# First chunk's projections and delta inside the stage ahead of each scan, and x kept by channels between scan layers

## The chip, the cores and the metric

The kernel runs on one core of one Trainium2 chip. The metric is the device time of one execution in microseconds (us). A core has five engines that each work through a queue of their own: TensorE (PE, with its weight loads as PEld), VectorE (DVE), ScalarE (ACT), GpSimd (POOL) and SyncE (SP), which here issues nearly all DMA transfers.

## What is computed

The input x has 4 images of 64 x 64 pixels with 96 channels. Two layers of a state-space model (layers 0 and 1) and two layers of linear attention with a quantised feed-forward network (layers 2 and 3, the token layers) follow each other, all with residuals:

```
x = x + conv(gn(x))          # layers 0 and 1; gn: mean and variance per group of 3 channels
t = t + attn(ln(t)); t = t + ffn(ln(t))    # layers 2 and 3

conv(v):                                   # D_INNER = 192, D_STATE = 16, K = 4 directions
  xp, z = split(v @ in_proj)               # 96 -> 2 * 192
  u  = silu(depthwise_conv3x3(xp) + bias)
  xs = u by rows, by columns, and both of these reversed
  dt, B, C = split(x_proj[k] @ xs[k])      # 6, 16 and 16 rows
  delta = softplus(dt_proj[k] @ dt + dt_bias[k])
  h[t] = exp(delta * A) * h[t-1] + (delta * u) * B[t]     # 16 states
  y[t] = sum over states of h[t] * C[t] + D * u
  y  = layernorm(sum of the 4 directions in image order) * w + b
  return (y * silu(z)) @ out_proj          # 192 -> 96
```

## The kernel before

**Units.** The images go in pairs, so each of layers 0 and 1 makes two units, four in all. The 192 inner channels of two images fill three groups of 128 partitions: `u0` and `u1` hold the first 128 channels of image 0 and 1, and `u2` the other 64 of both. For each unit `between_scans` runs a stage that makes the unit's `u` and, beside it, turns the scan's result of the unit before into x (`scan_outputs`). Then `scan_pair` runs the scan. After the fourth unit `token_layers` makes the last unit's outputs and layers 2 and 3.

**The stage.** `scan_inputs` is a generator. `turn(i)` (L171) loads image i in 8 pieces `xt` of 512 tokens, turns each by four TensorE transposes into `tps`, copies it to `xn` (ACT, L183) and takes its statistics (`bn_stats`, DVE, L184). Two tiny matmuls `gm` and `gv` sum them over a group of channels. `project(i, c)` (L202) then works on 512 tokens: the norm on VectorE in place (L207), three matmuls `ips` (L211; each shows as two records in the trace), copies into a padded image `img` and into `zs`, which is stored as `zg`. The convolution is split. `conv_product` (L144) does 512 positions by 9 matmuls `cps` with diagonal weights, and `conv_chain` (L155) does 1024 positions by 9 steps on VectorE (one `tensor_scalar`, L164, and eight `scalar_tensor_tensor`, L166), each with a SiLU on ScalarE. There are 8 products (18 records each in the trace) and 8 chains in a stage:

```
    for c in range(8):
        project(1, c)
        if c in (2, 5, 7):
            conv_chain(0, {2: 0, 5: 16, 7: 32}[c])
    for n in range(8):
        conv_product(*((1, 8 * n) if n < 6 else (0, 8 * n)))
        if n % 2:
            conv_chain(2, 8 * n - 8)
    conv_chain(1, 48)
```

**The outputs.** `scan_outputs` (L243) works on 16 groups of 256 tokens of both images. It loads `zt`, `ys` and the residual `xr`, takes layer norm statistics (`ystats`, `ymv` on DVE; the inverse root `ln_rs` on POOL, L81), normalises on ACT, transposes (`pt`, L292), scales (`gt`, ACT, L294), multiplies with silu(z) (`gt`, DVE, L301), multiplies with the output weights (`po`, L305 and L306), adds the residual (`xo`, DVE, L308) and stores. Two steps of `scan_inputs` follow each group.

**Order.** In stages and token layers a scheduler orders each engine's queue from the instructions' dependences and estimated costs. Within a scan the written order is kept: `InOrder` passes each instruction through L71, which is why the trace shows L71 for all of them.

**The scan.** `scan_pair` (L326) works on chunks of T = 1024 positions: 4 directions, 4 chunks, 3 partition groups, 48 steps. For each chunk `project` makes `xps` (x_proj), its copy `cdt`, the DRAM rows `crow`, `bt`, and a split of B in three bf16 parts (`parts`, `rest`, `bparts`). For each step `discretise` makes `delta` (softplus), `du` = delta * u (POOL) and its transpose `dut`. Both run ahead of the steps that need them, in between the scan's own work. Only for the first chunk nothing runs ahead, and before the loop stands (L602):

```
        for _ in begin_project(0, 0):
            pass
        for _ in begin_discretise(0):
            pass
```

The scan's own work is `da` = exp(delta * A) (ACT), `bp` (PE, DVE), the scan instruction `h` (DVE), `h` times the broadcast rows `cb` (POOL; `cb` and `bb` come by DMA from `crow`), and the sum `yp` (PE).

Of the kernel before, what the change touches and what calls it, by code (L numbers as in the profile page):

```python
# [84 lines left out]
class ScanLayer:  # L85


    def __init__(self, tc, pw, dram, ident, x_src, x_dst, w, n):
        nc = tc.nc
        self.x_src, self.x_dst, self.w = x_src, x_dst, w  # L90

        self.zg = [dram.tile([3, 128, L], F32, name=f"zg{n}{pr}") for pr in range(NB // 2)]
        self.y = [dram.tile([2, L, DI], F32, name=f"y{n}{pr}") for pr in range(NB // 2)]
        self.par = par = pw.tile([128, 2, P_ALL], F32, name=f"par{n}")
        nc.sync.dma_start(out=par, in_=w["par"].rearrange("s p c -> p s c"))

        self.amat = pw.tile([128, 2, K * NS], F32, name=f"amat{n}")
        nc.scalar.activation(self.amat, par[:, :, P_A : P_A + K * NS], AF.Exp)
        nc.vector.tensor_scalar(self.amat, self.amat, -1.0, None, ALU.mult)
        self.dsum = pw.tile([128, 2, 1], F32, name=f"dsum{n}")  # L100
        nc.vector.tensor_reduce(self.dsum, par[:, :, P_D : P_D + K], mybir.AxisListType.X, ALU.add)


def between_scans(tc, cst, ident, half, u, before, after):


    with ExitStack() as stage:
        ins = scan_inputs(tc, stage, cst, ident, half, u, *after)
# [10 lines left out]
def scan_inputs(tc, stage, cst, ident, half, u, layer, pr):  # L119
# [49 lines left out]
    xns, norms = [], []  # L169

    def turn(i):  # L171

        xn = pa.tile([C, L], F32, name="xn", tag=f"xn{i}")
        xns.append(xn)
        stats = p2.tile([C, 8, 6], F32, name="stats")
        for g in range(8):
            xt = p2.tile([128, 4, C], F32, name="xt")
            at = (2 * pr + i) * L + g * 512
            nc.sync.dma_start(out=xt, in_=x_src[at : at + 512, :].rearrange("(j p) c -> p j c", p=128))
            ps = pp.tile([C, 512], F32, name="tps", tag="mm")  # L180
            for j in range(4):
                nc.tensor.transpose(ps[:, 128 * j : 128 * j + 128], xt[:, j], ident)
            nc.scalar.copy(xn[:, 512 * g : 512 * g + 512], ps)  # L183
            nc.vector.bn_stats(stats[:, g], ps)  # L184
# [17 lines left out]
    def project(i, c):  # L202
# [4 lines left out]
        nc.vector.tensor_scalar(xns[i][:, cols], xns[i][:, cols], *norms[i], ALU.subtract, ALU.mult)  # L207
        pss = []
        for q in range(3):
            ps = pp.tile([128, 8, HW], F32, name=f"ips{q}", tag="mm")  # L210
            nc.tensor.matmul(ps, wi[:, i, 128 * q : 128 * q + 128], xns[i][:, cols], start=True, stop=True)  # L211
# [10 lines left out]
    for i in range(2):  # L222
        yield from turn(i)
    for c in range(8):
        project(0, c)
        if c % 2:
            yield
    for c in range(8):
        project(1, c)
        if c in (2, 5, 7):  # L230
            conv_chain(0, {2: 0, 5: 16, 7: 32}[c])
        if c % 2:
            yield
    for n in range(8):
        conv_product(*((1, 8 * n) if n < 6 else (0, 8 * n)))
        if n % 2:
            conv_chain(2, 8 * n - 8)
        yield
    conv_chain(1, 48)
    yield  # L240


def scan_outputs(tc, stage, ident, half, layer, pr, pp, turned="pt", summed="po"):  # L243
# [3 lines left out]
    p2 = stage.enter_context(tc.tile_pool(name="c2", bufs=3))  # L247
# [3 lines left out]
    for g in range(NT // 2):  # L251
# [3 lines left out]
        xr = p2.tile([128, 2, 2, C], F32, name="xr")  # L255
# [3 lines left out]
        for i, to, of in (  # L259
# [6 lines left out]
            )  # L266
        for i in range(2):
            there = (2 * pr + i) * L + at
            nc.sync.dma_start(
                out=xr[:, :, i], in_=x_src[there : there + 256, :].rearrange("(t p) c -> p t c", p=128)  # L270
            )
# [30 lines left out]
        po = pp.tile([128, 2, 2, C], F32, name="po", tag=summed, bufs=1 if summed == "po" else None)  # L302
        for t in range(2):
            for i in range(2):
                nc.tensor.matmul(po[:, t, i], gt[:, i, t], wo[:, 0], start=True, stop=False)  # L305
                nc.tensor.matmul(po[:, t, i], gt[:, 2, t], wo[:, 1 + i], start=False, stop=True)  # L306
        xo = p2.tile([128, 2, 2, C], F32, name="xo")
        nc.vector.tensor_tensor(xo, xr, po, ALU.add)  # L308
        for i in range(2):
            there = (2 * pr + i) * L + at  # L310
            nc.sync.dma_start(
                out=x_dst[there : there + 256, :].rearrange("(t p) c -> p t c", p=128), in_=xo[:, :, i]
            )
# [12 lines left out]
def scan_pair(tc, pk, cst, ident, u, first_weights, layer, pr):  # L326

    nc = InOrder(tc)
    par, amat, dsum, w, y = layer.par, layer.amat, layer.dsum, layer.w, layer.y[pr]
    with ExitStack() as stage:  # L330
        p2 = stage.enter_context(tc.tile_pool(name="b_2", bufs=2))
        pm = stage.enter_context(tc.tile_pool(name="b_ps", bufs=1, space=PSUM))
        pd = stage.enter_context(tc.tile_pool(name="b_d", bufs=2, space=DRAM))

        sel, ident16 = cst["sel"], cst["ident16"]

        def part(t, tr, c):

            v = t.rearrange("p (h w) -> p w h", w=HW) if tr else t.rearrange("p (h w) -> p h w", w=HW)
            return v[:, 16 * c : 16 * c + 16]  # L340

        weights = {0: first_weights}
# [5 lines left out]
        def project(k, uv):  # L348


            wx = weights[k][0]
            bparts = p2.tile([NP, T], BF16, name="bparts")
            cdt = p2.tile([NC, T], F32, name="cdt")
            crow = pd.tile([ND, T], F32, name="crow")
            bt = p2.tile([128, T // 128, 2 * NS], F32, name="bt")
            projected.append((uv, bparts, crow, cdt, bt))
            for hf in range(2):
                for j in range(3):
                    yield hf, 8 + 2 * j
                    if j == 0:  # L360
                        ps = pm.tile([NC, 512], F32, name="xps", tag="m1")
                    nc.tensor.matmul(ps, wx[:, j], uv[j][:, 8 * hf : 8 * hf + 8], start=(j == 0), stop=(j == 2))
                yield hf, 14
                nc.scalar.copy(cdt[:, 512 * hf : 512 * hf + 512], ps)
            nc.sync.dma_start(out=crow, in_=cdt[:ND])
            yield 2, 6
            ps = pm.tile([128, T // 128, 2 * NS], F32, name="btps", tag="m1")
            for t in range(T // 128):
                nc.tensor.transpose(ps[:, t], cdt[BR, 128 * t : 128 * t + 128], ident[BR, BR])

            parts = p2.tile([128, T // 128, 3, 2 * NS], BF16, name="parts", bufs=1)
            rest = p2.tile([128, T // 128, 2 * NS], F32, name="rest", bufs=1)
            yield 2, 8
            nc.scalar.copy(bt, ps)
            nc.scalar.copy(parts[:, :, 0], ps)
            nc.vector.tensor_tensor(rest, ps, parts[:, :, 0], ALU.subtract)
            yield 2, 10
            nc.scalar.copy(parts[:, :, 1], rest)
            yield 2, 10
            nc.gpsimd.tensor_tensor(parts[:, :, 2], rest, parts[:, :, 1], ALU.subtract)  # L380
            yield 2, 12
            ps = pm.tile([NP, T], BF16, name="bpps", tag="m1")
            for t in range(T // 128):
                nc.tensor.transpose(
                    ps[:, 128 * t : 128 * t + 128], parts[:, t].rearrange("p s n -> p (s n)"), ident16
                )
            yield 2, 14
            nc.scalar.copy(bparts, ps)
            yield None

        def discretise(k, j, uv, cdt):

            wdt = weights[k][1]
            bias = par[:, j // 2, P_DTB + k : P_DTB + k + 1]
            delta = p2.tile([128, T], F32, name="delta")
            du = p2.tile([128, T], F32, name="du")
            dut = p2.tile([128, T // 128, 128], F32, name="dut")
            made.append((delta, du, dut))
            halves = [slice(512 * hf, 512 * hf + 512) for hf in range(2)]
            pss = []  # L400
            for hf, cols in enumerate(halves):
                yield 2 * hf
                ps = pm.tile([128, 512], F32, name="dps", tag=f"m{hf}")
                nc.tensor.matmul(ps, wdt[ND:, j], cdt[ND:, cols], start=True, stop=True)
                pss.append(ps)
            yield 4
            for ps, cols in zip(pss, halves):
                nc.scalar.activation(delta[:, cols], ps, AF.Softplus, bias=bias)
            yield 6
            nc.gpsimd.tensor_tensor(  # L410
                du.rearrange("p (a b) -> p a b", b=HW), delta.rearrange("p (a b) -> p a b", b=HW), uv[j], ALU.mult
            )
            for hf in range(2):
                yield 10 + 2 * hf
                ps = pm.tile([128, 4, 128], F32, name="dups", tag="m0")
                for t in range(4):
# [614 lines left out]
```

## Time and profile before

| what | value |
|---|---|
| median of 3 runs | 10735.83 us (10733.38 to 10756.34) |
| the profiled execution's own time | 10738.98 us |
| its span in the trace | 10737.1 us |
| busy in the span | PE 76%, DVE 89%, ACT 82%, POOL 84% |
| stage ahead of the first scan | 0 to 168.2 us |
| stages between scans | 2473.1 to 2714.4, 5005.4 to 5250.2, 7543.1 to 7786.2 us |
| token layers, with the last unit's outputs | 10081 to 10737 us |

A stage between scans is counted from the last `h` product of a scan to the first scan instruction of the next. PEclk is the share of full TensorE clock that was granted. In the views shown below, a line gives start, duration, engine, source line, operation and tiles; `x8` is a count of instructions. A chain of waits is the thread of work and waits that ended last in a window, followed back from its end.

### The profile page before, as it was taken

The page shows a single profiled execution, that of the slowest core. Times are in us where ns is not written, and L with a number is a line of the kernel's source. Part 1 is how long each engine was busy: PE and PEld are TensorE (multiplying, and loading weights), DVE is VectorE, ACT ScalarE, POOL GpSimd, SP SyncE. Part 2 cuts the span into 40 slices and gives each one's busy share as a digit, 9 for nine tenths or more (in the row PEclk, how much of TensorE's full clock was granted, in tenths as well). Part 3 has the DMA queues.
Part 4 walks back from the last instruction along what each step waited for, and adds up shares of the span by engine and source line. Part 5 has one row for each costly group of instructions (what it writes and reads, how often), then busy time and mean ns, then how long its engine had stood idle before and what let it go on. Part 6 is the DMA issues. An engine that isn't in the chain of part 4 may idle for free.

```text
span 10737.1 us, 143300 instructions
## 1 busy us (share of the span) xinstructions
PE 8117.2 (76%) x48032; PEld 6033.3 (56%) x48032; DVE 9607.7 (89%) x6898; ACT 8780.3 (82%) x18807; POOL 9031.2 (84%) x5306
## 2 busy tenths in 40 slices
PE   7777777777777777776877777777777777777666
PEld 4555555554555555555555555555455555555554
DVE  7999999997899999998799999999699999999755
ACT  6988888885888888886788888888598888888656
POOL 3999999993899999996499999999299999999645
PEclk9888899888888898998888888898888889889877
DMA  3677777775577777777467777777566777777610
GB/s 123 208 211 216 215 225 218 214 217 149 187 209 218 217 220 222 217 220 193 150 207 210 221 217 220 223 215 219 142 195 212 212 216 220 222 217 216 187 32 24
DMA packets 960474, 2114.19 MB, mean 197 GB/s; under 512 B 413526, under 2 KB 704664, under 8 KB 762008
## 3 DMA queue, kind: packets, MB, share of 16 engines
q1 hardware_dynamic: 959736, 2105.01, 67.6%
q8 instruction: 382, 6.26, 0.3%
q14 instruction: 356, 2.92, 0.1%
HBM read 1943.27 MB, written 161.48 MB: 196 GB/s over the span
## 4 chain that ended last, share of the span: by engine, by line
ACT 35%; PE 19%; DVE 18%; issue 18%; POOL 8%; DMA 1%; SPq 1%; DVEq 0%; POOLq 0%; ACTq 0%
ACT x L71 15%; ACT da L71 13%; DVE h L71 10%; PE yp L71 6%; POOL h L71 5%; PE bp L71 5%; DVE bp L71 4%; ACT bp L71 2%; DVE u L166 2%; PE xps L71 2%; PE dps L71 1%; ACT L71 1%; PE dups L71 1%; DMA cb<-crow 1%; PE cps L150 1%
## 5 line engine op out<-in xcount | busy, mean ns | idle before, releaser
L71 POOL TENSOR_TENSOR h<-h,cb 128x1024 f32<-128x1024 f32 x3072 | 7194.5, 2366 | 233.3 <-issue 59.8
L71 DVE TENSOR_TENSOR_SCAN h<-da,last,bp 128x1024 f32<-128x1024 f32 x2064 | 4736.7, 2335 | 145.6 <-PE bp L71 23.6
L71 ACT ACTIVATE x<-dut,bt 128x128 f32<-128x128 f32 x12288 | 3495.2, 370 | 1.3 <-PE bp L71 0.8
L71 PE MATMUL yp<-ident,h 128*128 128x128 f32 x24576 | 3357.2, 296 | 10.2 <-POOL h L71 10.2
L71 PEld LDWEIGHTS yp<-ident,h 128*128 128x128 f32 x24576 | 3183.8, 156 | 125.3 <-issue 74.5
L71 ACT ACTIVATE da<-delta,amat 128x1024 f32<-128x1024 f32 x2752 | 3060.2, 1138 | 97.5 <-DVE h L71 96.4
L71 PE MATMUL bp<-ident,x 128*128 128x128 f32 x10240 | 1678.2, 316 | 1290.8 <-DVE h L71 938.6
L71 PEld LDWEIGHTS bp<-ident,x 128*128 128x128 f32 x10240 | 1361.5, 163 | 1851.0 <-ACT x L71 1036.8
L71 DVE TENSOR_TENSOR bp<-du,bp 128x1024 f32<-128x1024 f32 x1472 | 1780.3, 1213 | 311.2 <-PE bp L71 309.2
L71 DVE TENSOR_TENSOR_SCAN h<-da,bp 128x1024 f32<-128x1024 f32 x688 | 1537.7, 2274 | 48.0 <-ACT da L71 8.5
L71 PE MATMUL bp<-bparts,sel 96*128 96x512 bf16 x2944 | 922.0, 399 | 759.1 <-DVE h L71 745.8
L71 PEld LDWEIGHTS <-sel 96*128 96x128 bf16 x2944 | 227.3, 100 | 1553.6 <-DVE h L71 1045.3
L71 ACT ACTIVATE bp<-delta,amat 128x1024 f32<-128x1024 f32 x320 | 358.1, 1119 | 527.9 <-DVE h L71 525.9
L71 POOL TENSOR_TENSOR dbu<-du,bb 128x1024 f32<-128x1024 f32 x320 | 755.2, 2360 | 0.0
L81 POOL TENSOR_TENSOR ln_rs<-ln_ve,half 128x4 f32<-128x4 f32 x64 | 89.7, 1402 | 575.5 <-DVE ln_ve L79 539.0
L71 DVE TENSOR_TENSOR_SCAN h<-bp,last,dbu 128x1024 f32<-128x1024 f32 x240 | 558.9, 2329 | 13.8 <-POOL dbu L71 12.5
L71 PE MATMUL xps<-u,wx 128*76 128x512 f32 x768 | 561.9, 821 | 5.7 <-ACT cdt L71 2.9
L71 POOL TENSOR_TENSOR du<-delta,u 128x1024 f32<-128x1024 f32 x192 | 506.2, 2637 | 21.6 <-ACT delta L71 21.6
L71 POOL COPY last<-h 128x2 f32<-128x2 f32 x1152 | 216.8, 188 | 346.6 <-DVE h L71 344.3
L71 ACT ACT_TABLE_LOAD x384 | 492.7, 1283 | 6.9
L71 PE MATMUL dps<-cdt,wdt 12*128 12x512 f32 x768 | 449.3, 666 | 0.0
L71 ACT COPY ysum<-yp 128x1024 f32<-128x1024 f32 x192 | 194.4, 1013 | 292.5 <-PE yp L71 292.5
(132 smaller groups left out, 6482.2 us busy)
## 6 DMA issues: line engine op xcount, KB each, us to landing
cb<-crow SPq DMA_DIRECT2D x1024, 1024.0 KB
cb<-crow SPq DMA_DIRECT2D x1024, 512.0 KB
bb<-crow SPq DMA_DIRECT2D x384, 256.0 KB
bb<-crow SPq DMA_DIRECT2D x128, 512.0 KB
y<-ysum SPq DMA_DIRECT2D x192, 256.0 KB
kept<-y SPq DMA_DIRECT2D x160, 256.0 KB
y<-ysum SPq DMA_DIRECT2D x64, 512.0 KB
zt<-zg SPq DMA_DIRECT2D x64, 384.0 KB
```

The lines of the kernel that those rows point to most:

```text
L71: return self.tc.keep_in_program_order(getattr(self.engine, op)(*args, **kwargs))
L81: nc.gpsimd.tensor_tensor(rs, ve, half, ALU.pow)
L150: nc.tensor.matmul(ps, diag[:, tap], v, start=(tap == 0), stop=(tap == 8))
L166: nc.vector.scalar_tensor_tensor(to, v, weight, to, ALU.mult, ALU.add)
```

## The change

`scan_pair` becomes a class `PairScan`. Its method `begin` makes the first chunk's `project` and the first step's `discretise` within `scan_inputs`, after two of the eight products and two of the eight chains, with the stage's PSUM buffers and under the scheduler. The tiles that even chunks and steps use live in a pool `s_q` that stays open from unit to unit; the odd ones are in a pool of the scan, one buffer each. `crow` too lives outside.

Between the layers x is kept as [image, channel, token]; the host hands it over so. `turn` becomes `measure`: `xt` is loaded as 96 channels x 512 tokens in two buffers, without transposes and copies, and is only measured. `project` loads the same piece again as `xn`, two buffers. In the outputs, `xr` comes by one transfer, `po` has channels on partitions (4 matmuls of 256 columns; the old 8 of 96), and one store is made. Layer 1's outputs are still by tokens, as the token layers want them: there `po` keeps its 8 matmuls, and four transposes add `xr` into it, so that a copy on ScalarE takes the place of the addition on VectorE. The outputs' tiles have two buffers (three before), but for the last unit.

```diff
-    def turn(i):
-        xn = pa.tile([C, L], F32, name="xn", tag=f"xn{i}")
...
+    def measure(i):
         stats = p2.tile([C, 8, 6], F32, name="stats")
         for g in range(8):
-            xt = p2.tile([128, 4, C], F32, name="xt")
...
-            for j in range(4):
-                nc.tensor.transpose(ps[:, 128 * j : 128 * j + 128], xt[:, j], ident)
-            nc.scalar.copy(xn[:, 512 * g : 512 * g + 512], ps)
-            nc.vector.bn_stats(stats[:, g], ps)
+            xt = p2.tile([C, 512], F32, name="xt", bufs=2)
+            nc.sync.dma_start(out=xt, in_=x_src[2 * pr + i, :, 512 * g : 512 * g + 512])
+            nc.vector.bn_stats(stats[:, g], xt)
...
-        nc.vector.tensor_scalar(xns[i][:, cols], xns[i][:, cols], *norms[i], ALU.subtract, ALU.mult)
+        xn = p2.tile([C, 512], F32, name="xn", bufs=2)
+        nc.sync.dma_start(out=xn, in_=x_src[2 * pr + i, :, cols])
+        nc.vector.tensor_scalar(xn, xn, *norms[i], ALU.subtract, ALU.mult)
...
     for c in range(8):
         project(1, c)
-        if c in (2, 5, 7):
-            conv_chain(0, {2: 0, 5: 16, 7: 32}[c])
+        if c == 2:
+            conv_chain(0, 0)
+        elif c == 5:
+            conv_chain(2, 0)
         if c % 2:
             yield
-    for n in range(8):
+    conv_product(1, 0)
+    conv_product(1, 8)
+    scan.begin(nc, pp)
+    yield
+    for n in range(2, 8):
         conv_product(*((1, 8 * n) if n < 6 else (0, 8 * n)))
-        if n % 2:
-            conv_chain(2, 8 * n - 8)
         yield
-    conv_chain(1, 48)
-    yield
+        conv_chain(*((0, 16), (0, 32), (2, 16), (2, 32), (2, 48), (1, 48))[n - 2])
+        yield
...
-    p2 = stage.enter_context(tc.tile_pool(name="c2", bufs=3))
+    p2 = stage.enter_context(tc.tile_pool(name="c2", bufs=3 if layer.last and pr else 2))
...
+        if not layer.last:
+            po = pp.tile([C, 2, 256], F32, name="po", tag=summed, bufs=bufs)
             for i in range(2):
-                nc.tensor.matmul(po[:, t, i], gt[:, i, t], wo[:, 0], start=True, stop=False)
-                nc.tensor.matmul(po[:, t, i], gt[:, 2, t], wo[:, 1 + i], start=False, stop=True)
...
+                for q, j in ((0, i), (1 + i, 2)):
+                    v = gt[:, j].rearrange("p t q -> p (t q)")
+                    nc.tensor.matmul(po[:, i], wo[:, q], v, start=(q == 0), stop=(q > 0))
+            xo = p2.tile([C, 2, 256], F32, name="xo")
+            nc.vector.tensor_tensor(xo, xr, po, ALU.add)
...
+        else:
...
+                    v = xr[:, i, 128 * t : 128 * t + 128]
+                    nc.tensor.matmul(po[:, t, i], v, ident[:C, :C], start=False, stop=True, is_transpose=True)
+            xo = p2.tile([128, 2, 2, C], F32, name="xo")
+            nc.scalar.copy(xo, po)
...
+    def begin(self, nc, pm):
+        for _ in self.project(nc, self.pq, pm, "mm", 0, 0):
+            pass
+        for _ in self.discretise(nc, self.pq, pm, ("mm", "mm"), 0):
+            pass
...
-        for _ in begin_project(0, 0):
-            pass
-        for _ in begin_discretise(0):
-            pass
```

## Prediction

> **What bounds the kernel now.** I read the page first (whole-kernel shares), then busy time over windows I chose for the stretches ahead of each scan, then the chain of waits in them. The page says that VectorE is busy 89%, GpSimd 84%, ScalarE 82% of the span; that belongs to the four scans, some 2300 us each, whose instructions the change leaves as they are, in the same written order. What moves lies in five windows: the stage ahead of the first scan (0 to 168.2 us), the three stages between scans (each from the last work of a scan to the first `h` scan of the next) and the token layers, where the last unit's outputs are made.
>
> ```profile
> core 0: us, PE busy (x) PEld busy (x) DVE busy (x) ACT busy (x) POOL busy (x), PEclk, DMA share, GB/s
> 0.00:168.20 168.20, 136.60 (x354) 64.11 (x354) 105.92 (x123) 70.86 (x114) 11.41 (x31) 0.96 0.31 91
> 2473.10:2714.40 241.30, 188.09 (x722) 108.61 (x722) 151.49 (x310) 124.21 (x240) 37.58 (x43) 0.86 0.49 138
> ...
> 7543.10:7786.20 243.10, 190.34 (x722) 110.59 (x722) 151.58 (x308) 124.19 (x240) 37.54 (x43) 0.85 0.49 137
> 10081.00:10737.00 656.00, 428.82 (x2928) 341.43 (x2928) 353.56 (x1252) 388.69 (x897) 299.18 (x362) 0.74 0.17 52
> ```
>
> First number: length of the window; then each engine's busy time. TensorE (PE) is the fullest engine in all of them, but no window is full. The chain of waits of 0 to 175 us (start, duration, what) says why:
>
> ```profile
> 38.27 44.10 PE ips L211 x96
> 82.37 61.82 PE cps L150 x144
> ...
> 144.96 2.81 PE xps L71 x6
> ...
> 153.43 0.44 DVE rest L71
> ...
> 159.77 2.35 POOL du L71
> ...
> 165.71 1.28 ACT L71
> 166.99 0.01 issue
> 167.00 1.15 ACT da L71
> ```
>
> TensorE runs unbroken from 38.3 to 144.2: in-projection, then the matmul half of the convolution. Then the first chunk's prologue (`xps` to `dut`, a table load, `da`) runs as one thread from hand to hand, 144.2 to 168.2. The VectorE half of the convolution ended at 128.9 and its engine then waits 24.5 us.
>
> A stage between scans has three phases. To 2542 us it is bound by latency: scan drain, `y` stores and the first output groups, about 12.8 us each. Then TensorE and VectorE are full together; last comes the prologue:
>
> ```profile
> 2552.00:2664.00 112.00, 109.95 (x366) 56.06 (x365) 104.79 (x171) 70.39 (x136) 17.25 (x9) 1.00 0.50 139
> ```
> ```profile
> 2688.00:2714.40 26.40, 16.31 (x42) 6.38 (x42) 1.69 (x4) 9.53 (x14) 3.00 (x2) 0.63 0.45 157
> ```
>
> In the second row only 16 of 26.4 us of TensorE are busy (at clock 0.63) and VectorE does 1.7 us. Prices for the full phase come from the groups of 2552 to 2664 (count, busy and mean ns):
>
> ```profile
> L166 DVE SCALAR_TENSOR_TENSOR u<-img,par,u 128x1024 f32<-128x1024 f32 x64 | 80.7, 1277 | 0.0
> L150 PE MATMUL cps<-img,diag 128*128 128x512 f32 x129 | 57.0, 593 | 0.0
> L81 POOL TENSOR_TENSOR ln_rs<-ln_ve,half 128x4 f32<-128x4 f32 x9 | 17.2, 1916 | 95.6 <-DVE ln_ve L79 83.4 <-ACT gt L294 8.4 <-ACT zs L217 3.7
> ```
>
> Records overlap, so I price by spacing: a tap on VectorE 1.20 us (64 of them fill 76.8 of the 112), a `cps` record 61.82/144 = 0.43, an `ips` record 44.1/96 = 0.46.
>
> **What the Trainium skill says.** "TensorE: Matmul & The Clock Gate", "Part 1: The HAM clock gate", puts an idle array at half clock and asks about 3.4 us of sustained work to release it: the trace shows 1.00 in the full phase and 0.63 over the prologue. "Part 4: PE-mode transpose" there gives about 275 ns for a transpose within a kernel; here a `pt` record took 0.27 us in the token layers at a low clock, and six took 0.82 us at full clock. "DMA: Bandwidth & Descriptors", "Anatomy of one DMA", gives a fixed 2.0 us; here buffer release to landing of `xt` took 2.5 to 2.8. "ScalarE: Activation LUTs", "What ACT_TABLE_LOAD costs", gives 1283 ns and a drain of 1380; here 1.28 at 165.71 with `da` 0.01 us later, so I add no drain.
>
> **The change, stage 0.** Everything is compared in each engine's written order. The prologue moves on TensorE's queue from behind all 16 half-products (8 products of 18 records) to behind the first two. TensorE is in order: where the prologue waits, the last six products wait too.
> - Start. 64 transposes and 16 copies go; x comes ready in a ring of two buffers, so each pair of loads costs release to landing 2.65 plus one `stats` 0.69, about 3.4 us, eight pairs 27 after the first landing at 12, plus 2 of group norm: `ips` starts at 41.6 (was 38.3): +3.
> - Projection. The norms `xn` now stand between chain taps on VectorE, about three taps a chunk in the second half, 4.1 us against TensorE's 2.76. The last norm falls at about 94, `ips` ends at 96.7 (was 82.4). Each norm also waits for its own 96x512 reload (16 more loads on SP, at 0.45 us an issue); the wait is hidden by the taps ahead of it if it is under 2.6 us.
> - Two products, 36 records: to 112.3. `xps` with its two copies to 118.7. `rest` needs VectorE, where 58 chain steps (50x1.20 + 8x0.75 = 66), 16 norms (8) and the statistics stand ahead: 49.1 + 71.7 = 120.8. So about 121.5, and by the old prologue's steps (153.4 to 165.1 less cold `dps`) `dups` ends at 132.4.
> - Then 108 records, 46.4, plus 1 to 2 of cold clock: 180. Last `u` silu 0.7, table 1.3, `da` 1.15: first scan at about 183, against 168.2: **+15**. Bounds +22 (norms really waiting) and 0 (TensorE undelayed in projection). Below that only if TensorE doesn't wait at all (rival one).
>
> **Stages 1 and 2.** 13.5 us of transposes and 9.6 of copies leave the latency phase; I take 6 of them as path (bounds 0 and 10): `ips` at 2536, VectorE full from 2544 (was 2552). Ahead of `rest` on VectorE stand 48 taps (57.6), 7 first taps (5.3), 14 norms (7.0), 18 `ystats`/`ymv` (6.2), 4 `gt` (3.5), 5 `xo` (2.4), small ones (1.0) and five stalls of 0.9 on POOL's `ln_rs`: 87.5, so `rest` at 2632. TensorE needs only `ips` 44.6, 15.5 of products and the outputs' share by then, and stands idle some 30 us. From `rest`, 11 to the last `dups`, then six products 46.4, four `po` 7.2, three `pt` 2.5: +67; the last group's `gt`, `po`, `xo`, the buffers' release and the table load 6, cold clock 2: `da` at 2707, against 2713.2: **-6** each. Bounds: -14, where the 30 us of idle are half filled, and +5. In the prologue POOL's `parts` and `du` now queue with `ln_rs`; each is at most 1.9 us late, within the bounds. Outputs have two buffers of each tile instead of three; once VectorE is full a group takes about 9 us and a load under 4, so I cost that at nothing; without that cover it is 1 to 2 us a group, 16 groups.
>
> **Stage 3.** The same, but `xo` leaves VectorE for ScalarE and each group gets four transposes: **-5**.
>
> **Scans.** `cb` can load only once the stage's buffers are free; before, it was under way in the prologue, and landed about 5 us after issue. The first `h` product comes 6.0 us after the first scan: +1 each, **+4** (0 to 12).
>
> **Token layers.** 16 groups in a loop of about 7.2 us whose chain is `pt`, `gt`, `gt`, `po`: four transposes of 0.13 (full clock) to 0.27 lengthen `po` by 0.5 to 1.1, `xo` passes from VectorE's 0.55 to ScalarE's similar copy, and one DMA issue of 0.47 on SP goes: **+8** (0 to +17).
>
> Sum on the profiled execution (span 10737.1, 10739.0 in all): 15 - 6 - 6 - 5 + 4 + 8 = **+10**. That execution is 3.2 above the median 10735.8, so 10746.
>
> **Rivals.** *The intended gain (faster).* TensorE never waits in the prologue, because VectorE reaches `rest` early. Stage 0 starts its scan at 41.6 + 44.6 + 61.8 + 9 + 3.5 = 160.5 (-8), the three stages gain the bound -14 each, scans and tokens +12: -38, **10698**. For it: 24 to 26 us of prologue stand alone now, four times. Against: the taps ahead of `rest` are on the fullest engine of the new order.
> *Slower.* One mechanism: a norm waits at the head of VectorE for its reload, in a ring of two that is freed only when six `ips` records have read it, with SP's queue of `zg` stores and output loads ahead of the issue. Every microsecond there delays `rest`, and all six products behind it. At 0.6 us for each of 16 norms the stages turn from -6 to about +4, stage 0 becomes +20, tokens at 12 and scans 4: +48, **10784**. It decides from about 0.24 us per norm (11 us over three stages). For it: SP issues at 0.45 us apiece and loads take 2.6. Against: taps of 1.2 us hide most of it.
> *It doesn't do what it says.* TensorE still waits through the whole prologue and only the order differs: stages 0, stage 0 +15, the rest as above: +27, **10763**.
>
> **How the numbers follow.** This kernel can tell about 0.2%, 21.5 us, from no change: 10714 to 10757. The sum lands inside (0.42). The gain has 0.20; the two slower cases, and the upper part of the costs' bounds, 0.38. The bounds together reach 10694 and 10802; 8 in 10 gives 10706 to 10790.
>
> **What would show it.** Right: in stage 0 a gap of TensorE of some 10 us after the second product, `rest` near 121 at the end of VectorE's taps, the first scan near 183; in stage 1 TensorE idle ahead of `rest` near 2632 and full after it, the first scan 4 to 8 us earlier, counted from the end of the scan before; token layers a few us longer. Wrong: `rest` well before VectorE's taps end, TensorE with no gap, stages shorter by over 14, or a longer scan.

## The result and the profile after

The changed kernel took 10749.79 us (median of 4 runs, 10739.48 to 10755.79), the kernel before 10734.6 (4 runs, 10713.61 to 10756.34). The ratio is 1.0013 with a 95% interval of 0.9991 to 1.0034: no difference that these runs can tell. The forecast was 10746. Its total was right by luck: its terms were wrong by up to 37 us each and cancelled, as the windows of the profiled execution show (span 10750.3; 10737.1 before):

| window, us | before | forecast change | after | change |
|---|---|---|---|---|
| ahead of the first scan | 168.2 | +15 | 198.1 | +29.9 |
| stage between scans 1 | 238.6 | -6 | 245.3 | +6.7 |
| stage between scans 2 | 242.2 | -6 | 246.2 | +4.0 |
| stage between scans 3 | 240.5 | -5 | 249.3 | +8.8 |
| scan 1 | 2307.6 | +1 | 2297.8 | -9.8 |
| scans 2 to 4, together | 6886.5 | +3 | 6889.2 | +2.7 |
| last unit's outputs and token layers | 653.5 | +8 | 624.5 | -29.0 |

A stage is counted here from the end of the last `h` product to the first scan instruction (before, 2475.8 to 2714.4 for the first), a scan from there to its last `h` product. The changes add to +13.3, and the two spans differ by 13.2.

Busy time by window, changed kernel; the columns are length, then busy time of each engine with its instructions, granted clock, DMA share and GB/s:

```profile
0.00:198.10 198.10, 124.86 (x290) 53.16 (x290) 105.75 (x122) 63.40 (x99) 25.10 (x31) 0.93 0.26 78
2495.90:2741.20 245.30, 186.05 (x522) 93.87 (x522) 155.32 (x308) 117.88 (x225) 34.58 (x42) 0.82 0.47 136
...
7581.80:7831.10 249.30, 195.24 (x714) 114.75 (x714) 146.81 (x293) 124.30 (x241) 35.16 (x41) 0.83 0.47 133
10125.80:10750.30 624.50, 401.47 (x2984) 317.23 (x2984) 344.93 (x1236) 393.60 (x913) 296.18 (x361) 0.79 0.17 53
```

TensorE is busy 11.7 us less in the first window, as 15.9 us of transposes left it, and yet the window is 30 us longer. GpSimd, 11.4 us before, is at 25.1. The timeline of the changed kernel's first stage says where both come from. First TensorE (start, duration, instructions; idle time before it and its releaser in brackets):

```profile
95.87 2.81 PE L209 MATMUL ips<-xn,wi 96*128 96x512 f32 x6 [1.23 <-DVE xn L205]
98.52 15.62 PE L153 MATMUL cps<-img,diag 128*128 128x512 f32 x36
113.97 5.31 PE L390 MATMUL xps<-u,wx 128*76 128x512 f32 x12
...
137.79 1.09 PE L412 MATMUL bpps<-ident,parts 128*96 128x128 bf16 x8 [17.40 <-POOL parts L408]
138.81 3.78 PE L434 MATMUL dps<-cdt,wdt 12*128 12x512 f32 x4
145.78 1.97 PE L447 MATMUL dups<-ident,du 128*128 128x128 f32 x8 [3.19 <-POOL du L440]
147.55 47.36 PE L153 MATMUL cps<-img,diag 128*128 128x512 f32 x108
```

Projection and two products end at 114, as forecast (112.3); then TensorE stands 17.4 us waiting for GpSimd's `parts`, with the other 108 records of the convolution behind it in its queue. On GpSimd and VectorE, in the same stretch:

```profile
123.37 14.37 POOL L408 TENSOR_TENSOR parts<-rest,parts 128x256 bf16<-128x256 f32 x1 [80.44 <-ACT parts L406]
```
```profile
122.45 0.40 DVE L404 TENSOR_TENSOR rest<-btps,parts 128x256 f32<-128x256 f32 x1
122.79 17.35 DVE L169 SCALAR_TENSOR_TENSOR u<-img,par,u 128x1024 f32<-128x1024 f32 x14
```

`rest` came at 122.45 (forecast 121.5). The next instruction, an operation that takes 0.67 us in the 60 chunks made within scans, took 14.37 while VectorE ran convolution taps (the `scalar_tensor_tensor` steps of a chain) back to back. The Trainium skill, "SBUF — State Buffer", "Who interferes with whom", says that a VectorE instruction with two SBUF inputs contends with a GpSimd instruction that reads SBUF, and that the loser blocks. A tap has two such inputs, `img` and `u`. The page speaks of one instruction's length; here the wait was about eleven taps long (13.7 us at 1.2 us each).

In the first stage between scans the order of events was as forecast, a little later at each step. TensorE again, and ScalarE at its end:

```profile
2634.18 15.62 PE L153 MATMUL cps<-img,diag 128*128 128x512 f32 x36
...
2662.20 1.09 PE L412 MATMUL bpps<-ident,parts 128*96 128x128 bf16 x8 [4.19 <-POOL parts L408]
...
2672.25 15.62 PE L153 MATMUL cps<-img,diag 128*128 128x512 f32 x36
```
```profile
2738.76 1.28 ACT L71 ACT_TABLE_LOAD   x1 [7.15 <-DMA x<-xo]
```

The projection had taken from 2556.5 to 2633.9, 77 us against 44.6 of `ips` work. From 2672 to 2731 TensorE is full with products and output matmuls. Then ScalarE, on the way to `da`, waits 7.15 us: `da` needs the memory of the outputs' tiles, and the last `po`, the addition and the last store of x come first.

### The profile page after: what moved, and what is told of

Read it like the earlier page. It is cut to its first block, busy times and chain, and to the rows that moved or that the text cites. A ratio compares the mean times of both kernels' runs of the same rounds, so it can differ in the third digit from the quotient of the medians.

```text
span 10750.3 us, 142469 instructions
## 1 busy us (share of the span) xinstructions
PE 8091.1 (75%) x47648; PEld 5985.1 (56%) x47648; DVE 9599.0 (89%) x6866; ACT 8765.2 (82%) x18779; POOL 9043.5 (84%) x5306
## 5 line engine op out<-in xcount | busy, mean ns | idle before, releaser
L71 DVE TENSOR_TENSOR_SCAN h<-da,bp 128x1024 f32<-128x1024 f32 x688 | 1537.5, 2274 | 53.3 <-ACT da L71 13.3
L71 PE MATMUL xps<-u,wx 128*76 128x512 f32 x720 | 532.9, 825 | 0.0
L71 ACT ACT_TABLE_LOAD x380 | 487.5, 1283 | 23.4 <-DMA x<-xo 16.7
```

The source lines that it names most:

```text
L71: return self.tc.keep_in_program_order(getattr(self.engine, op)(*args, **kwargs))
```

## Experiments

One profile was taken of each variant. Windows are named as in the table above. Where an edit doesn't reach, they repeat within about 1 us for the first stage, 2 us for the first two stages between scans, 5 us for the third (249.3 and 254.1), and up to 13 us for a scan (the second took 2291.3 to 2304.7).

**The third bf16 part on VectorE.** In `project`, for the first chunk only:

```diff
-        for _ in self.project(nc, self.pq, pm, "mm", 0, 0):
+        for _ in self.project(nc, self.pq, pm, "mm", 0, 0, nc.vector):
...
-        nc.gpsimd.tensor_tensor(parts[:, :, 2], rest, parts[:, :, 1], ALU.subtract)
+        (third or nc.gpsimd).tensor_tensor(parts[:, :, 2], rest, parts[:, :, 1], ALU.subtract)
```

> The changed kernel with one edit: in the first chunk's prologue alone, the third bf16 part (parts minus rest) is made on VectorE and not on GpSimd. In the changed kernel that GpSimd instruction took 14.37 us in stage 0 (0.67 us elsewhere), while VectorE ran convolution taps back to back. Theory (a tap, with two operands in SBUF, keeps GpSimd's instruction from reading for as long as taps follow each other): bpps on TensorE starts about 13.5 us earlier and the first scan at about 184.5 us in place of 198.1; stages 1 to 3 gain 1 to 2.6 us each. Rival (the prologue waits in stage 0 for something else that ended at 137.8): the first scan stays at 197 to 199.

First scan at 191.9: `bpps` started at 124.96, 12.8 us earlier, but only 6 us arrived at the end. The next GpSimd instruction of the prologue had met the taps in its turn, as GpSimd's timeline of this run shows; in the changed kernel it took 2.34.

```profile
130.56 8.51 POOL L440 TENSOR_TENSOR du<-delta,u 128x1024 f32<-128x1024 f32 x1 [87.56 <-ACT delta L438]
```

Stages between scans: 241.1, 247.9, 245.9. The stall is shown, the size of the gain was over-stated.

**No GpSimd in the prologue.** `du` of the first step on VectorE too.

> The changed kernel with both GpSimd instructions of the first chunk's prologue, parts and du, made on VectorE. With parts alone moved, du took 8.51 us in stage 0 (2.34 elsewhere): it ran into the taps in its turn, and the first scan came at 191.9. Theory (two-operand taps keep GpSimd from reading): du takes about 1.2 us on VectorE behind at most two taps, dups ends some 7 us earlier and the first scan starts at about 185 us; stages between scans 1 to 2 us under the changed kernel's 245.3, 246.2 and 249.3. Rival (du was late for another reason): 190 to 192 us.

First scan at 183.1, 15.0 us earlier than in the changed kernel. That is the 13.7 us of the stall, and the rest is near what VectorE saves by being quicker at both (`parts` 0.42 us for 0.67, `du` 1.22 for 2.34). Stages 245.5, 242.3, 248.7, a gain of 0 to 4 us. In those stages taps stand between other instructions, and in the changed kernel `parts` took 2 to 3.3 us there.

**The prologue put back into the scan.** The call of `begin` leaves the stage; `project` and `discretise` run ahead of the scan's loop, on its PSUM tags.

> The changed kernel with the first chunk's prologue put back to the start of the scan (x by channels, the order of products and chains and all else stay). Theory (TensorE's queue is what the prologue holds up, so the move costs as much as it hides): stage 0 starts its scan at about 184 (changed kernel 198.1, before 168.2), because TensorE runs all 144 records of the convolution from 98.5 to 160.3 and 24 us of prologue follow; stages between scans take 238 to 242 us (changed 245.3, 246.2, 249.3). Rival (the move pays, and x by channels costs): stages 255 to 265 us, 10 to 20 longer than in the changed kernel. After the last scan both expect about 625 us, as in the changed kernel (624.5; before 653.5).

First scan at 185.7, as the theory had it. The stages took 246.6, 245.8 and 251.4, which neither side expected. So, with everything else as changed, moving the prologue out of the scan is worth 1.3, -0.4 and 2.1 us in the stages and costs 12.4 in the first one; with no GpSimd in it (the run before this one) the first one gains 2.6. The last convolution records of the first stage, in this run and in the changed kernel, show why it is worth so little:

```profile
2689.13 4.46 PE L153 MATMUL cps<-img,diag 128*128 128x512 f32 x10
```
```profile
2723.20 4.46 PE L153 MATMUL cps<-img,diag 128*128 128x512 f32 x10
```

Counted from the end of the scan before, the convolution ends at 214.4 us with the prologue in the scan and at 231.7 with it in the stage, 17.3 later. From the last `xo` to the scan it is then 23.4 us in the one and 4.7 in the other. So what no longer stands at the end is given back on TensorE's way to it. What made the windows longer than before (the first one by 17.5 us, the stages by 4 to 11) is then the rest of the change: x by channels with its rings, its order of work and the outputs' two buffers. After the last scan it took 626.1.

**Four buffers for xn.** One number:

```diff
-        xn = p2.tile([C, 512], F32, name="xn", bufs=2)
+        xn = p2.tile([C, 512], F32, name="xn", bufs=4)
```

> The changed kernel with four buffers for xn in place of two. Theory (the norms stand behind taps because each waits for its reload in a ring of two): the projection in stage 0 ends about 5 to 8 us earlier than 98.5, and in the stages between scans it takes some 70 us instead of 77; the prologue's GpSimd stall stays, so the first scan comes at 190 to 196 and the stages gain 3 to 6 us. Rival (the norms are late because taps were put ahead of them and VectorE is full): projection and stages as before within 2 us.

Stages 231.6, 232.9, 234.3: 13.7, 13.3 and 15.0 us shorter, about three times what the theory expected. TensorE's line of the first stage shows what happened, and GpSimd's why nothing of it arrived there:

```profile
42.20 43.69 PE L209 MATMUL ips<-xn,wi 96*128 96x512 f32 x96
```
```profile
112.35 22.98 POOL L408 TENSOR_TENSOR parts<-rest,parts 128x256 bf16<-128x256 f32 x1 [69.18 <-ACT parts L406]
```

The projection is one unbroken run that ends at 85.9 and not at 98.5. But `parts`, ready earlier, met more taps and took 23 us, so the first scan came at 196.9. VectorE's timelines show how the ring acts. In the changed kernel, from the 14th of the 16 norms on:

```profile
87.11 0.54 DVE L205 TENSOR_SCALAR xn<-xn,mean,gn_rs 96x512 f32<-96x512 f32 x1
87.56 3.66 DVE L169 SCALAR_TENSOR_TENSOR u<-img,par,u 128x1024 f32<-128x1024 f32 x3
91.15 0.54 DVE L205 TENSOR_SCALAR xn<-xn,mean,gn_rs 96x512 f32<-96x512 f32 x1
91.60 3.66 DVE L169 SCALAR_TENSOR_TENSOR u<-img,par,u 128x1024 f32<-128x1024 f32 x3
```

With four buffers, the last three norms, and in the kernel before the last eight:

```profile
75.11 0.54 DVE L205 TENSOR_SCALAR xn<-xn,mean,gn_rs 96x512 f32<-96x512 f32 x1
75.57 3.67 DVE L169 SCALAR_TENSOR_TENSOR u<-img,par,u 128x1024 f32<-128x1024 f32 x3
79.16 0.54 DVE L205 TENSOR_SCALAR xn<-xn,mean,gn_rs 96x512 f32<-96x512 f32 x1
79.62 1.27 DVE L169 SCALAR_TENSOR_TENSOR u<-img,par,u 128x1024 f32<-128x1024 f32 x1
80.81 0.54 DVE L205 TENSOR_SCALAR xn<-xn,mean,gn_rs 96x512 f32<-96x512 f32 x1
```
```profile
39.13 3.74 DVE L207 TENSOR_SCALAR xn<-xn,mean,gn_rs 96x512 f32<-96x512 f32 x8 [0.68 <-POOL gn_rs L81]
```

In the changed kernel VectorE is never idle in this stretch, so it isn't that a norm waits at the queue's head for its reload (idle time on `xn`'s transfer came to 2.0 us in the whole projection of the first stage between scans). Chain steps have been put ahead of the norms, two or three for each, and TensorE needs a norm every 2.76 us. With four buffers no chain step stands ahead of the first five norms, and 22 chain steps stand ahead of the last norm where it was 34. Twelve taps of 1.2 us are 14.4 us, and the last norm came that much earlier, at 80.8 and not at 95.2. In the kernel before, which had all of x in SBUF and no such ring, no chain step stood between the norms. So the theory was right that the ring is the cause, and the rival right in how the delay looks.

**Four buffers for xn, prologue in the scan.**

> The changed kernel with four xn buffers and the prologue put back into the scan. With the ring of four alone (prologue in the stage) the windows were 196.9 for stage 0 and 231.6, 232.9, 234.2 between scans. Theory (with TensorE no longer kept waiting by the norms, hiding the prologue pays what of it is now exposed): stage 0 at 86 + 62 + 24 = 172, stages 240 to 248, so the move is worth 8 to 15 us in each stage and costs 25 in stage 0 by the GpSimd stall. Rival (the move pays nothing in the stages, as the runs with a ring of two had it): 231 to 235.

First scan at 171.5 (172 expected), but stages of 232.9, 235.6, 236.9: the rival was right. With the ring repaired, the move as the change makes it is worth 1.3, 2.8 and 2.6 us in the stages (against the run before this one) and costs 25.4 us in the first. In all 10693.42 us, ratio to the kernel before 0.9968 (0.9956 to 0.9980).

**The prologue's pieces between the products**, without GpSimd. `begin` becomes a generator, and so many of its steps are taken ahead of each product:

```diff
-    scan.begin(nc, pp)
+    first = scan.begin(nc, pp)
     yield
     for n in range(2, 8):
+        for _ in range((9, 4, 6, 3, 40, 0)[n - 2]):
+            next(first, None)
         conv_product(*((1, 8 * n) if n < 6 else (0, 8 * n)))
```

> As the run with no GpSimd instruction in the prologue, and the prologue's pieces are written between the last six products of the convolution (xps ahead of the third, btps and the split ahead of the fourth, bpps and dps ahead of the fifth, dups after it), so that TensorE has a product to do while each hand-over is under way. Theory (the prologue costs because TensorE's queue waits in it): stage 0 is TensorE-bound from the first product at 98.5 on, 61.8 of convolution and about 9 of prologue, last record at 169 to 171, first scan at 173 to 176 us (before 168.2, changed 198.1); stages between scans about 10 us shorter than in the changed kernel, 235 to 239. Rival (in the stages VectorE or the outputs set the end, not TensorE): stage 0 as said, stages still 243 to 249.

First scan at 172.3; TensorE's timeline of the first stage has no gap left from 97.7 on:

```profile
113.17 5.31 PE L390 MATMUL xps<-u,wx 128*76 128x512 f32 x12
118.32 7.89 PE L153 MATMUL cps<-img,diag 128*128 128x512 f32 x18
126.14 0.68 PE L397 MATMUL btps<-ident,cdt 32*128 32x32 f32 x8
126.75 7.99 PE L153 MATMUL cps<-img,diag 128*128 128x512 f32 x18
134.58 0.61 PE L412 MATMUL bpps<-ident,parts 128*96 128x128 bf16 x8
```

Stages 241.6, 241.1 and 242.2, 4 to 7 us shorter: between theory and rival. Why not more is open; the slow projection doesn't explain it, since with four buffers for `xn` the same step brings no more (again 4 to 7 us, from 231.6, 232.9, 234.3 to the 226.7, 229.1, 227.8 of the run "All mended").

**Three buffers for the outputs' tiles in all units.**

> The changed kernel with three buffers for the outputs' tiles in all units, as before. Theory (the first output groups wait for their buffers: the load of xr stands on SP behind the store of x): each stage between scans gets 3 to 6 us shorter (245.3, 246.2, 249.3 in the changed kernel). Rival (they wait for the chain of hands within a group): within 1.5 us.

Stages 248.0, 248.1, 239.0. Neither theory: the first two are 2 to 3 us longer, about what such windows repeat to, and only the third, in which layer 1's outputs are made, is 10.3 us shorter. Why that one alone was not tried. The traces show one difference: in the third stage alone SP stands waiting with the loads of `xr` for `po`, which there reads `xr` too (33.0 us in six waits with two buffers, 24.7 in two with three).

**The token layers.** The -29 us are 17 in the outputs' loop and 12 after it. Two runs look into them. In the kernel before, the last unit's residual goes through TensorE and ScalarE (`summed` is "po" in all other units):

```diff
-                nc.tensor.matmul(po[:, t, i], gt[:, 2, t], wo[:, 1 + i], start=False, stop=True)
+                nc.tensor.matmul(po[:, t, i], gt[:, 2, t], wo[:, 1 + i], start=False, stop=summed == "po")
+                if summed != "po":
+                    nc.tensor.matmul(po[:, t, i], ident, xr[:, t, i], start=False, stop=True)
...
-        nc.vector.tensor_tensor(xo, xr, po, ALU.add)
+        if summed != "po":
+            nc.scalar.copy(xo, po)
+        else:
+            nc.vector.tensor_tensor(xo, xr, po, ALU.add)
```

> The kernel before with one edit in the last unit's outputs: xr is added into po by one more matmul with the identity (4 a group), and ScalarE copies xo; VectorE's addition goes. Loads and stores stay as before. Theory (the outputs' loop in the token layers became shorter because the addition left VectorE and TensorE's clock stays up): the loop takes about 5.8 us a group in place of 6.8, and the time from the last h product to the end falls from 653.5 to about 635. Rival (it became shorter because xr comes by one transfer of longer rows): 6.8 us a group, 650 to 656 us. The three stages between scans and the first one are untouched: 238.6, 242.2, 240.5 and 168.2 us, which also shows how far such windows repeat.

In the changed kernel, the last unit's `xr` in two transfers:

```diff
-            nc.sync.dma_start(out=xr, in_=x_src[2 * pr : 2 * pr + 2, :, at : at + 256].rearrange("i c t -> c i t"))
+        if layer.last and pr:
+            for i in range(2):
+                nc.sync.dma_start(out=xr[:, i], in_=x_src[2 * pr + i, :, at : at + 256])
+        else:
+            nc.sync.dma_start(out=xr, in_=x_src[2 * pr : 2 * pr + 2, :, at : at + 256].rearrange("i c t -> c i t"))
```

> The changed kernel with the residual xr of the last unit loaded by two transfers, one an image, in place of one; rows stay as long. In the kernel before (two xr loads of 384-byte rows) the outputs' loop took 6.8 us a group, and 6.7 when the addition alone left VectorE; in the changed kernel 5.75. Theory (SP's number of issues paces the loop): about 6.3 to 6.8 us, the time after the last scan 8 to 16 us over 625. Rival (the longer rows of the load by channels): 5.75 us and 625.

| | last scan to last `xo`, us | mean from one `xo` to the next, us | rest, us | clock in the rest |
|---|---|---|---|---|
| before | 154.5 | 6.73 | 499.0 | 0.74 |
| before, addition on TensorE | 154.9 | 6.64 | 487.5 | 0.78 |
| after | 137.4 | 5.58 | 487.1 | 0.78 |
| after, two `xr` loads | 145.7 | 6.14 | 500.5 | 0.74 |
| after, four buffers for xn, prologue in the scan | 144.7 | 6.05 | 488.0 | 0.79 |

The rows behind them: kernel before, changed kernel, the run with two loads, and the first row of the last run (from the last scan to the last `xo`, and from there to the end):

```profile
10083.60:10238.10 154.50, 91.75 (x572) 81.12 (x573) 67.92 (x292) 82.69 (x193) 34.81 (x38) 0.72 0.54 150
10238.10:10737.10 499.00, 335.98 (x2350) 259.45 (x2349) 285.64 (x960) 306.00 (x704) 261.77 (x323) 0.74 0.05 20
```
```profile
10125.80:10263.20 137.40, 84.78 (x639) 76.08 (x639) 60.77 (x276) 88.13 (x209) 34.19 (x38) 0.80 0.60 169
10263.20:10750.30 487.10, 316.69 (x2348) 241.15 (x2346) 284.16 (x960) 305.47 (x705) 261.98 (x323) 0.78 0.05 21
```
```profile
10122.60:10268.30 145.70, 88.44 (x636) 80.34 (x637) 60.76 (x276) 88.59 (x209) 34.24 (x38) 0.78 0.56 160
10268.30:10768.80 500.50, 336.73 (x2350) 259.88 (x2349) 285.81 (x960) 306.37 (x705) 262.89 (x323) 0.74 0.05 20
```
```profile
10053.10:10197.80 144.70, 90.40 (x639) 80.89 (x640) 60.40 (x276) 88.37 (x209) 34.22 (x37) 0.76 0.57 161
```

The outputs' loop doesn't shorten when the addition leaves VectorE. With one load more on SP it was 8.3 us longer, but that SP's number of issues paces the loop is not shown. Ten profiles have the changed kernel's last unit as it is, and their loops took 137.2 to 144.7 us: the longest, in the last line of the table, had one load a group and came within 1 us of the run with two. The 17 us against the kernel before are clear of this spread; what made them (an issue less, the longer rows of `xr`, or something else) was not taken apart. The rest of the token layers does the same instructions in 486 to 490 us at a granted TensorE clock of 0.77 to 0.79 in twelve of the fourteen profiles, and in 499 or 500 us at 0.74 in the other two, the kernel before and the run with two loads.

> The kernel before with the last unit's addition on TensorE and ScalarE, once more and timed. Its first profile had the part after the last output 487.5 us long at a granted clock of 0.78, against 499.0 at 0.74 in the kernel before; the run with two xr loads, which adds on TensorE too, had 500.5 at 0.74. Theory (the addition on TensorE raises the clock for what follows): again about 488 us, the median about 11 us under the kernel before, ratio 0.9990. Rival (the clock after the outputs falls one way or the other by chance or by the loop's timing): a ratio of 1.000 within 0.0005, or a profile with 499.

The repeat had 487.5 at 0.78 again, and 642.4 us after the last scan in both; but the median, 10725.97 against 10732.07, gave a ratio of 0.9994 (0.9985 to 1.0002), an interval that takes in both forecasts. What picks the level stays open, since the run with two loads adds on TensorE too and had the low clock.

**All mended:** no GpSimd in the prologue, its pieces between the products, four buffers for `xn`, three for the outputs' tiles of layer 1.

> The changed kernel with what the earlier runs point to: the prologue without GpSimd and its pieces between the products, four buffers for xn, and three buffers for the outputs' tiles of layer 1 (with three buffers in all units the stage of layer 1's first outputs alone became shorter, 238.9 for 249.3). Theory (the parts add, since TensorE is the bound in all of them): in stage 0 the projection ends at 86, the last record at about 157, the first scan starts at 160 to 163 us; stages between scans 225 to 232; 626 after the last scan; in all about 10655 to 10675, ratio to the kernel before 0.993 to 0.995. Rival (with TensorE free, VectorE sets the end in the stages, so the ring's gain and that of the spread prologue don't add): stages 230 to 235, in all 10680 to 10700.

First scan at 160.8, stages 226.7, 229.1, 227.8. Against the changed kernel the stages lost 18.6, 17.1 and 21.5; the ring alone and the spread prologue alone had 17.4, 18.5 and 22.0 together, so they add; in the third stage the 10 us of the outputs' third buffer did not come on top. 10664.61 us, ratio 0.9938 (0.9926 to 0.9951).

**And three buffers for xt.**

> As the mended kernel, with three buffers for xt. Theory (the ring of two in the measuring phase sets the start of the projection in stage 0 at 41.6): three buffers start it 5 to 8 us earlier, first scan at 153 to 157 us; in the stages between scans the measuring stands behind the output groups on SP, so within 2 us. Rival (the loads' own issue and order set it): within 1.5 us of the mended kernel everywhere.

First scan at 153.5; stages 219.2, 224.4 and 234.9, of which the last is longer and the others shorter than expected. 10638.88 us, ratio to the kernel before 0.9917 (0.9903 to 0.9930): faster than both kernels. Its first stage, for the row of the changed kernel above:

```profile
0.00:153.50 153.50, 118.51 (x290) 52.52 (x290) 106.65 (x124) 62.72 (x99) 8.38 (x29) 1.00 0.34 101
```

## Why the prediction was right in its sum and wrong in its terms

- **Stage 0, up to `rest`: right.** `ips` from 41.97 (41.6 forecast) to 98.5 (96.7), products to 114 (112.3), `rest` at 122.45 (121.5), behind the 58 chain steps that had been counted. That TensorE's queue is what the prologue holds up is shown by the run with its pieces between the products: 172.3, and 183.1 without that.
- **Stage 0, from `rest` to `dups`: the step that failed there.** It took over the old prologue's steps, 11 us, with `parts` at 0.67 us. In the old place VectorE was idle; in the new one it runs taps. `parts` took 14.37, and `dups` ended at 147.6 and not at 132.4. For the stages between scans I had noted that GpSimd's `ln_rs` takes 1.9 us beside taps, and put "at most 1.9 us late" on `parts` and `du`; in stage 0, where the taps follow each other without a break, I put nothing on them. The 13.7 us that `parts` took longer and the 1 us by which `rest` was late are nearly all of the missing 15.
- **Stages between scans: sign wrong, -17 forecast, +19.5 measured.** The 6 us from the latency phase came (`ips` 60.5 us after the scan, 66.2 before). The sum of VectorE's work ahead of `rest` was 90.2 us for 87.5. But full VectorE started 71.8 us after the scan, not 68.4; `rest` to the end of the `dups` took 14.5 for 11; and from there to the scan it took 69 for 65, with `da`'s 7.15 us of waiting in it, which I had put at a share of 6 with the last `gt`. These are small terms of one sign. The larger error was to take the order, norms behind taps, as given: the ring of two makes it, and four buffers take 13 to 15 us out of each stage. The outputs' two buffers, which I had put at nothing, cost 10.3 us in the third stage (three buffers: 239.0 for 249.3) and nothing that shows in the first two. My slower rival named that ring and its size: it turned the stages from -6 to +4, and +6.7, +4.0, +8.8 were measured. Its mechanism was wrong in one point: the norms don't wait on the engine, the order written for it does.
- **Scans: +4 forecast, -7 measured.** Scan 1 took 2307.6, 2307.8 and 2307.8 us in the three profiles with x by tokens, and 2291 to 2298 in all eleven with x by channels, whether the prologue stood in it or not. The cause was not found; scans 2 to 4 changed by 2.7 us together, within what they repeat to.
- **Token layers: +8 forecast, -29 measured.** The loop was forecast to lengthen by 0.5 us a group and became 17 us shorter in all. The 0.5 to 1.1 us a group that I had put on the added work of TensorE don't show: the kernel before took 154.5 us without the addition on TensorE and 154.9 with it. (The 0.27 us that I read for a `pt` record there was the shortest of 96; their median is 0.33.) Which term makes the 17 us stays open. The other 12 us come after the outputs and go with the granted clock there, for which I had no term.
- **The intended gain** was under the named rival's price: moved as the change does it, the prologue brings at most 2.8 us a stage. That is near the third rival's price for the stages, nothing; but TensorE does not wait through the whole prologue there, as that rival had it, its convolution ends later. With its pieces between the products, no GpSimd in it and a ring of four, it brings, against the prologue in the scan, 6 to 7 us in the first two stages and 11 in stage 0 (9 in the third stage, where the outputs' third buffer is in as well).

## What to carry to other kernels

When a thread of small steps moves beside other work, take each step's time from a place where that same work runs beside it; a hand-over through an engine that shares its access with a busy one can cost twenty times its own time. Put the thread's pieces between pieces of the work that shares its queue, so that nothing stands behind a wait. A ring's depth acts on the order that a scheduler writes long before anything is seen to wait for it, so look at what stands between two uses of the ring as well as at the waits. And compare windows, not totals: here a total within 0.04% of the forecast hid errors of 11 to 37 us.

## What the runs showed of the hardware

A GpSimd `tensor_tensor` on SBUF of 0.67 us took 14.4 and 23.0 us, and one of 2.34 us took 8.5, while VectorE ran two-operand taps of 1.2 us back to back: by these lengths, an estimate, it lost not one turn but some five to twenty. Where other instructions stood between the taps, the first took 0.9 to 3.3 us. And the same token-layer instructions ran in 486 to 490 us with a granted TensorE clock of 0.77 to 0.79, or in 499 to 500 us with 0.74.
